# Attention over pooled maps and a large-kernel convolution: GpSimd's early 2x2 sums moved to the third chunk, partial products copied back two steps ahead

## The chip, the cores and the metric

The kernel runs on one core of a Trainium2 chip. The metric is the device time of one execution in microseconds (us). Four runs of the kernel before gave 3069.72 to 3074.2 us, with a median of 3070.95. All matrices are float32.

## The reference

The input x is 384 channels of 192x192. Two layers follow each other, each added to its input. `_gn` is a group norm over 32 groups of 12 channels, each over the whole image.

```
# layer 0
qkv = einsum(gn(x), w_qkv) + b_qkv          # 384 -> 3*384 channels, 192x192
qkv = max over 2x2 cells                    # 96x96
qkv = depthwise 3x3 convolution + b_dw
q, k, v = split; q, k normalized over the 96*96 positions
attn = einsum(q, k) per head (48x48, 8 heads)
out = sum of 4 softmaxes, each over the top 24, 32, 36, 38 of a row, times v
out = gelu(out), repeated 2x2, projected by w_proj + b_proj
x = x + out
# layer 1
x = x + sum of 7 depthwise convolutions of gn(x) (13x13 and smaller), each with its scale and shift
```

The change touches only the start of layer 0: the group norm's statistics, which need all of x, and the first products with w_qkv that are made while those statistics still run.

## The kernel before

**Stages.** (1) Statistics: all of x is read once and its mean and variance are taken by channel. (2) The main loop of layer 0: x is read again in bands of eight image rows (B, 24 bands, each in two halves sb of four rows), normalized, multiplied with w_qkv on TensorE (`project`, line 615), reduced by 2x2 maxima on VectorE (`pool`, line 627), and convolved 3x3 on VectorE (`taps`, line 663); q and k in a first pass, v in a second. (3) Attention and projection. (4) The large convolution on TensorE (line 1297). The stages from (1) to the end of (2) are written with a manual schedule: each engine executes its instructions in the order in which the program emits them. An engine that waits for a semaphore holds up everything behind it in its queue, DMA issues included.

**The statistics.** The first two bands (`NKEEP` = 2) come through the tiles `xts`. The rest of each chunk of 128 channels (chunks 1, 2 and 3 in this document, j = 0, 1, 2 in the code) is cut into NX = 22 pieces of 128x1536, so n = 0 to 65 counts the pieces of all three chunks, with j, b = divmod(n, 22): chunk 2 is n = 22 to 43, chunk 3 is n = 44 to 65. The loop over n does the following for each piece:
- It takes the piece's statistics: three `bn_stats` on VectorE (line 476), or, in chunks 1 and 2 for b = 4, 7, 10, 13, 16 and 19, two passes of ScalarE, one for the sum and one for the square (lines 472 and 473).
- It gives the piece's buffer back and issues the load of a later piece into the buffer that is the oldest free one (`load_blocks`, line 310). Eight such buffers go round, three in the memory of `v` and five called `xs`; so from n = 34 on, piece n takes the buffer that piece n - 8 has left (n = 26 to 33 take those of n - 12, since four pieces ahead of them go to places of their own). From n = 8 on, loads of even n are issued by SP, those of odd n by GpSimd.
- It advances the merging of the convolution weights on GpSimd (`merge`), and for each odd n it calls `sum_one`.

At the end of a chunk, `bn_aggr` (line 505) joins the statistics; for chunks 1 and 2 VectorE then reads what ScalarE has summed up (line 510).

**The early work.** With chunk 1's statistics done, the groups that lie in it are known, and its channels of early pieces can be normalized. `ready` (line 387) normalizes one piece of 128 channels by 4 image rows on ScalarE, and appends it to the list `early_sums`. `first_chunk`, advanced by one step after each `bn_stats` of chunk 2, normalizes the channels of chunk 1 of bands 2 to 5 and of both halves of bands 0 and 1, eight pieces, multiplies those of bands 2 to 5 with the q and k weights (m = 0, 1, 2; `multiply`, line 398) and copies each partial product from PSUM to SBUF (`put_by`, line 409). `early`, advanced in the same way in chunk 3, does so for the channels of chunk 2: eight more pieces, and 18 products (`EARLY`: bands 0 to 5, m = 0 to 2). For bands 0 and 1 (the first NKEEP * NJ = 6 steps) it multiplies both chunks at once. For bands 2 to 5 the product that was put by must be copied back into PSUM first (`fill`, line 246), the new one is accumulated on it, and the result is put by again. Once the group values are there, `early` emits all steps up to n = 15 without a pause and yields True, which sets `going`; the last two steps (LATE = 2) are emitted after the loop, around the statistics of the third chunk's groups. PSUM has two buffers of this kind (`qkvps`, bufs=2), which `multiply`, `fill` and the main loop's `project` share.

**The 2x2 sums.** Layer 1 needs 2x2 sums of the normalized x. `sum_one` takes the oldest entry of `early_sums` and calls `sum_up`: three additions on GpSimd (lines 257 to 259) into one of two small buffers at the end of `v`'s memory, taken in turn, and a DMA issued by GpSimd that writes 96 KB to `sums` (line 261). There are 16 entries in all. What is left after the loop is summed in `while early_sums: sum_one()`, which stands behind the nine memsets of the tiles `pooled` (line 578) and ahead of the main loop's own work for GpSimd.

**The end of the stage.** `group_stats` computes the last groups' mean and variance with small matmuls (lines 112, 123 and 147), a square root on ScalarE (line 90), and VectorE's steps between; then ScalarE normalizes the third chunk of band 0 (line 456), the first product is filled back (line 246), and the main loop begins on TensorE (line 615).

Of the kernel before, what the change touches and what calls it, by code (L numbers as in the profile page):

```python
# [16 lines left out]
NJ = C // P  # L17
# [40 lines left out]
def tile_attn_then_large_kernel_conv(ctx: ExitStack, tc: tile.TileContext, a: dict, out: bass.AP):  # L58
# [149 lines left out]
    NKEEP = 2  # L208
    EARLY = [(B, m) for B in range(6) for m in range(NJ)]
# [26 lines left out]
    def halved(t):  # L236
        return t.rearrange("p (r w) -> p r w", r=SR)

    filled = []

    def fill(B, m, sb):


        if sb == 0 and (B, m) in begun:
            ps = qkvps.tile([P, SR, 512], F32, tag="qkv", name="qkv")
            nc.scalar.copy(ps[:, :, : 2 * W], halved(begun[B, m]))  # L246
            filled.append(ps)
# [20 lines left out]
    with (  # L268
# [28 lines left out]
        def load_blocks():  # L297

            while waiting:
                n = waiting[0]  # L300
                j, b = divmod(n, NX)
                if (j, b) in kept:
                    xs = kept[j, b]
                elif ring:
                    xs = ring.pop(0)
                else:
                    return

                eng = nc.scalar if n < 8 else nc.gpsimd if n % 2 == 1 else nc.sync
                eng.dma_start(out=xs, in_=x[j * P : (j + 1) * P, FX + b * FB : FX + (b + 1) * FB])  # L310
                xss[waiting.pop(0)] = xs
                if len(xss) == 2:
                    yield
# [57 lines left out]
        def sum_one():  # L371
            if early_sums:
                t, B, sb, j = early_sums.pop(0)
                o = NJ * HS * WS - (len(early_sums) % 2 + 1) * SR * WS
                sum_up(free[:, o : o + SR * WS].rearrange("p (r w) -> p r w", r=SR), t, B, sb, j)


        def rows_stats(n):
            xt = xts[n // 2, n % 2]
            for j in range(NJ):  # L380
                nc.vector.bn_stats(stats[:, j, 2 * n, :], xt[:, j, :512])
                nc.vector.bn_stats(stats[:, j, 2 * n + 1, :], xt[:, j, 512:])

        def ready(B, sb, j):

            t = xts[B, sb][:, j] if B < NKEEP else kept[j, B - NKEEP][:, :HB]
            nc.scalar.activation(t, t, AF.Identity, bias=gn0[:, j, 1:2], scale=gn0[:, j, 0:1])
            early_sums.append((t, B, sb, j))
            pieces[B, sb, j] = t

        def multiply(B, m, js, ps=None):

            start = ps is None
            if start:
                ps = qkvps.tile([P, SR, 512], F32, tag="qkv", name="qkv")
            for r in range(SR):
                for j in js:
                    nc.tensor.matmul(  # L398
                        ps[:, r, : 2 * W],
                        lhsT=wqk[:, j, m * P : (m + 1) * P],  # L400
                        rhs=pieces[B, 0, j][:, r * 2 * W : (r + 1) * 2 * W],
                        start=(start and j == js[0]),
                        stop=(j == js[-1]),
                        skip_group_check=not start,
                    )
            return ps

        def put_by(B, m, ps):
            nc.scalar.copy(halved(begun[B, m]), ps[:, :, : 2 * W])
# [22 lines left out]
        def early():  # L432

            pc = yield from group_stats(s1, s_ps, mvx, "ge", gw, terms[1:6], (1,), True)
            yield
            nc.vector.tensor_copy(gn0[:, 1], pc[:, 1])
            ready(0, 0, 1)
            ahead = None
            for n, (B, m) in enumerate(EARLY):
                if m == 0 and B < EARLY[-1][0]:  # L440
                    ready(B + 1, 0, 1)
                ps = multiply(B, m, (0, 1)) if B < NKEEP else multiply(B, m, (1,), ahead)
                if n + 1 < len(EARLY) and EARLY[n + 1][0] >= NKEEP:
                    fill(*EARLY[n + 1], 0)
                    ahead = filled.pop()
                if n == len(EARLY) - 1:
                    yield True
                put_by(B, m, ps)
                if n < NKEEP:
                    ready(n, 1, 1)  # L450
                if n >= len(EARLY) - LATE - 1:
                    yield True
# [4 lines left out]

        early_sums, pieces = [], {}
        begin, first = first_chunk(), early()
        going = False  # L460
        pivot = s1.tile([P, 2, 2], F32, name="pivot")
        acc = s1.tile([P, 2, len(BY_ACT), 2], F32, name="acc")
        done = [NS0] * NJ
        for n in range(NJ * NX):
            if n in (1, 3, 5, 7):
                rows_stats(n // 2)
            j, b = divmod(n, NX)
            xt = xss.pop(n)
            if j < 2 and b in BY_ACT:

                sums2 = acc[:, j, BY_ACT.index(b)]
                nc.scalar.activation(xt, xt, AF.Identity, bias=pivot[:, j, 0:1], accum_out=sums2[:, 0:1])
                nc.scalar.activation(xt, xt, AF.Square, accum_out=sums2[:, 1:2])
            else:
                for q in range(FB // 512):
                    nc.vector.bn_stats(stats[:, j, done[j], :], xt[:, q * 512 : (q + 1) * 512])  # L476
                    done[j] += 1
                    if j == 1:
                        next(begin, None)
                    if j == 2 and not going:  # L480
                        going = next(first)
                if j < 2 and b == 0:
                    nc.vector.bn_aggr(pivot[:, j], stats[:, j, NS0 : done[j]].rearrange("p n s -> p (n s)"))
                    nc.vector.tensor_scalar(pivot[:, j, 0:1], pivot[:, j, 0:1], -1.0, None, ALU.mult)
            if (j, b) not in kept:
                ring.append(xt)
            for _ in load_blocks():
                pass
            next(merging, None)
            if n % 2 == 1:  # L490
                sum_one()
            if j < 2 and b == NX - 16:
                w = P * (j + 1)
                nc.scalar.dma_start(
                    out=spares[j], in_=x[w : w + MORE[j], :].rearrange("c (k n) -> (c k) n", k=P // MORE[j])
                )
                nc.scalar.dma_start(out=wqk[:, j, :C], in_=wqkv[:, j, :C])
            if j < 2 and b == NX - 6:
                k = HW * MORE[j] // P // 384
                sy = stats[:, j, -k:]  # L500
                for q in range(k):
                    nc.vector.bn_stats(sy[:, q, :], spares[j][:, q * 384 : (q + 1) * 384])
                nc.vector.bn_aggr(mvx[:, 3 * j, :], sy.rearrange("p n s -> p (n s)"))
            if b == NX - 1:
                nc.vector.bn_aggr(
                    mvx[:, (1, 4, 6)[j], :], stats[:, j, : done[j]].rearrange("p n s -> p (n s)")
                )
                if j < 2:
                    m = mvx[:, 3 * j + 2, :]
                    nc.vector.tensor_reduce(m, acc[:, j].rearrange("p n s -> p s n"), AX.X, ALU.add)  # L510
                    nc.vector.tensor_scalar(m, m, 1.0 / len(BY_ACT) / FB, None, ALU.mult)
                    t = s1.tile([P, 1], F32, name=f"sq{j}")
                    nc.vector.tensor_mul(t, m[:, 0:1], m[:, 0:1])
                    nc.vector.tensor_sub(m[:, 1:2], m[:, 1:2], t)
                    nc.vector.tensor_sub(m[:, 0:1], m[:, 0:1], pivot[:, j, 0:1])
# [24 lines left out]
    with ctx_v:  # L540
# [380 lines left out]
        with ctx_m:  # L921
# [4 lines left out]
            for s, (B, u, m, sb) in enumerate(steps):  # L926
# [8 lines left out]
                ps = project(B, m, sb)  # L935
                if s + 1 < len(steps):
                    n = steps[s + 1]
# [8 lines left out]
                if B + 1 < 2 * NB:  # L946
                    ahead = (u - 6,) if B < NB else (2 * u - 6, 2 * u - 5)
# [38 lines left out]
        with (  # L986
# [31 lines left out]
            with tc.manual_schedule():  # L1018
# [22 lines left out]
                for b in range(NBB):  # L1041
# [6 lines left out]
                    for c in range(NPR):  # L1048
                        k = P if c < NJ else P2
                        ps = b1_ps.tile([P, NBK], F32, tag=f"av{c}", name="av")  # L1050
# [293 lines left out]
        with (  # L1344
# [4 lines left out]
            with tc.manual_schedule():  # L1349
                for n in range(NJ * NBB):  # L1350
# [6 lines left out]
                    ps = b2_ps.tile([P, NBK], F32, tag="pj", name="pj")  # L1357
# [62 lines left out]
    with (  # L1420
# [5 lines left out]
        with tc.manual_schedule():  # L1426
# [4 lines left out]
            for k in range(NK):  # L1431
# [6 lines left out]
                for c in range(CC):  # L1438
# [13 lines left out]
                    n = c - (CC - 3 if k == 0 else 3)  # L1452
# [54 lines left out]
```

## Time and profile before

| | |
|---|---|
| median of 4 runs | 3070.95 us (3069.72 to 3074.2) |
| profiled execution, its time | 3070.8 us |
| its span in the profile | 3068.7 us |
| mean granted clock of TensorE | 0.993 |
| busy over the span: PE, DVE, ACT, POOL | 96%, 82%, 44%, 30% |
| first matmul of the main loop (line 615) | 177.66 us |
| 16 sums of early pieces, DMA issues (line 261) | 81.6 to 167.9 us |
| time from such an issue to its landing, least, median, most | 1.9, 5.9, 10.7 us |
| loads of line 310 from issue to landing, least, median, most | 4.4, 11.2, 26.4 us |

Times inside the execution count from the start of the span. PE is TensorE, PEld its loading of weights, DVE VectorE, ACT ScalarE, POOL GpSimd and SP the engine that issues most DMAs; a q behind a name (SPq, ACTq) is that engine's queue issuing a DMA. In lists in order of time, the first number is the start, the second the length. "a<-b" names what is written and what is read. The chain that ended last is followed back from the last instruction, at each step to what released it. Idle time ahead of an instruction is put down to the releaser that came last by the profile; where the engine named had long been done, it was another.

### The profile page before, as it was taken

Reading aid. Unit: us, or ns where it says so; the run is one execution under the profiler, and the core shown is the slowest. Engines: PE = TensorE matmul, PEld = TensorE weight load, DVE = VectorE, ACT = ScalarE, POOL = GpSimd, SP = SyncE. Lnnn points to the kernel's source line nnn. Section 1 sums busy time; section 2 is a strip of 40 time slices with the busy share of each in tenths; the row PEclk is TensorE's granted clock in tenths of the full one; section 3 lists DMA queues with packets and bytes.
Section 4 is the critical chain, followed back from the end, with each engine's and each line's share of the span. In section 5 each row is a group of like instructions: output and inputs, shape, how many; then the busy total and the mean of one; then the engine's idle time right before and its main releaser. Section 6 shows DMA issues by size and latency. Waiting matters only on the chain.

```text
span 3068.7 us, 32213 instructions
## 1 busy us (share of the span) xinstructions
PE 2932.4 (96%) x10842; PEld 1944.3 (63%) x10842; DVE 2515.9 (82%) x3483; ACT 1336.0 (44%) x2457; POOL 932.4 (30%) x1147
## 2 busy tenths in 40 slices
PE   0699999999999999999999999999999999999998
PEld 0355556666666666666555555555777877777776
DVE  6778897878888887888999899888788777777775
ACT  2655554444444444444444444733333333333332
POOL 4422132332323232412222222500433333333332
PEclk9899999999999999999999999999999999999999
DMA  9943342424333333333333332587999999999994
GB/s 386 379 158 95 131 155 77 154 88 146 96 134 102 132 114 120 128 107 110 103 101 101 129 105 70 170 230 205 267 268 243 245 243 245 245 244 246 245 220 118
DMA packets 275924, 525.73 MB, mean 171 GB/s; under 512 B 25954, under 2 KB 190480, under 8 KB 275632
## 3 DMA queue, kind: packets, MB, share of 16 engines
q1 hardware_dynamic: 204432, 326.44, 40.0%
q0 software_dynamic: 49376, 174.29, 17.5%
q10 hardware_dynamic: 21952, 22.95, 2.2%
q8 instruction: 86, 1.41, 0.2%
q14 instruction: 78, 0.64, 0.1%
HBM read 362.23 MB, written 161.37 MB: 171 GB/s over the span
## 4 chain that ended last, share of the span: by engine, by line
PE 84%; DVE 10%; DMA 3%; issue 2%; ACT 1%; POOL 0%; ACTq 0%; SPq 0%; POOLq 0%; DVEq 0%
PE qkv L615 45%; PE conv L1297 29%; PE pj L1359 4%; DVE v L663 3%; DVE acc L663 2%; PE av L1051 2%; DVE mx L627 2%; PE gram L704 2%; PE tr L692 2%; DMA v<-in_x 1%; DVE stats L476 1%; DMA xt<-in_x 1%; PE qkv L398 1%; DMA xs<-in_x 0%; DVE xp L1279 0%
## 5 line engine op out<-in xcount | busy, mean ns | idle before, releaser
L615 PE MATMUL qkv<-xt,wqk 128*128 128x384 f32 x3312 | 1087.6, 487 | 6.1 <-ACT qkv L246 5.5
L1297 PE MATMUL conv<-xp,wt 128*128 128x288 f32 (+1 forms) x3840 | 917.7, 402 | 2.2 <-ACT co L1305 2.2
L615 PEld LDWEIGHTS qkv<-xt,wqk 128*128 128x128 f32 x3312 | 621.1, 190 | 425.4 <-ACT qkv L246 12.2
L1297 PEld LDWEIGHTS conv<-xp,wt 128*128 128x128 f32 x3840 | 729.8, 190 | 187.8 <-ACT co L1305 2.6
L663 DVE SCALAR_TENSOR_TENSOR acc<-pooled,wd,acc 128x384 f32<-128x384 f32 (+2 forms) x1152 | 731.5, 635 | 30.5
L634 ACT ACTIVATE pooled<-mx,bq 128x192 f32<-128x192 f32 x432 | 196.8, 455 | 921.2 <-DVE mx L627 919.8
L627 DVE TENSOR_REDUCE mx<-qkv 128x192 f32<-128x768 f32 x432 | 412.1, 954 | 210.3 <-PE qkv L615 194.1
L1279 DVE STREAM_TRANSPOSE xp<-xn 128x4608 f32<-128x4608 f32 (+1 forms) x107 | 441.8, 4129 | 166.5 <-PE conv L1297 158.2
L615 PE MATMUL qkv<-xt,wv 128*128 128x384 f32 x1728 | 563.7, 487 | 1.7 <-ACT xt L596 1.1
L615 PEld LDWEIGHTS qkv<-xt,wv 128*128 128x128 f32 x1728 | 325.8, 190 | 234.1 <-ACT xt L596 7.5
L1305 ACT ACTIVATE co<-conv,cb 128x288 f32<-128x288 f32 x384 | 191.1, 499 | 598.8 <-PE conv L1297 588.6
L663 DVE SCALAR_TENSOR_TENSOR v<-pooled,wd,v 128x384 f32<-128x384 f32 (+2 forms) x576 | 375.4, 652 | 15.1
L257 POOL TENSOR_TENSOR sum<-xt 128x192 f32<-128x192 f32 x128 | 87.5, 684 | 957.1 <-ACT xt L596 944.6
L1322 POOL DMA_DIRECT2D out<-o x191 | 105.8, 583 | 569.3 <-DVE o L1313 514.5
L596 ACT ACTIVATE xt<-xt,gn 128x768 f32<-128x768 f32 x278 | 275.4, 1014 | 0.0
L1256 POOL TENSOR_TENSOR raw<-raw,up 128x2496 f32<-128x2496 f32 x46 | 230.8, 5017 | 24.6 <-DMA up<-pd 23.0
L1313 DVE STREAM_TRANSPOSE o<-co 128x2304 f32<-128x2304 f32 (+1 forms) x50 | 210.0, 4204 | 19.8 <-ACT co L1305 19.8
L732 POOL DMA_DIRECT2D zd<-v x96 | 72.0, 757 | 240.6 <-ACT v L723 239.9
L1359 PE MATMUL pj<-v,wp 128*128 128x384 f32 x432 | 142.5, 489 | 0.9 <-ACT gx L1062 0.6
L1359 PEld LDWEIGHTS pj<-v,wp 128*128 128x128 f32 x432 | 81.1, 190 | 55.5 <-ACT gx L1062 1.2
L1264 ACT ACTIVATE xn<-raw,par 128x2112 f32<-128x2112 f32 x48 | 102.9, 2144 | 3.3 <-POOL raw L1256 1.7
L258 POOL TENSOR_TENSOR sum<-sum,xt 128x192 f32<-128x192 f32 x128 | 100.9, 789 | 10.8
(284 smaller groups left out, 1918.0 us busy)
## 6 DMA issues: line engine op xcount, KB each, us to landing
xt<-in_x SPq DMA_DIRECT2D x96, 1152.0 KB, 7.6
wt<-zd SPq DMA_DIRECT2D x46, 1536.0 KB, 13.8
raw<-in_x SPq DMA_DIRECT2D x182, 312.0 KB, 13.8
out<-o POOLq DMA_DIRECT2D x188, 288.0 KB, 7.2
zd<-v POOLq DMA_DIRECT2D x96, 416.0 KB, 4.6
up<-pd SPq DMA_DIRECT2D x184, 156.0 KB, 12.5
xs<-in_x POOLq DMA_DIRECT2D x20, 768.0 KB, 10.6
smj<-sums SPq DMA_DIRECT2D x72, 192.0 KB, 3.0
```

Source lines behind the costliest of these rows:

```text
L596: nc.scalar.activation(xt[:, j], xt[:, j], AF.Identity, bias=gn0[:, j, 1:2], scale=gn0[:, j, 0:1])
L615: nc.tensor.matmul(ps[:, r, : 2 * W], lhsT=wq[:, j, mm * P : (mm + 1) * P], rhs=xt[:, j, r * 2 * W : (r + 1) * 2 * W], start=(j == 0), sto ...
L627: nc.vector.tensor_reduce(mx, ps[:, :, : 2 * W].rearrange("p r (y w x) -> p r w y x", y=2, x=2), AX.XY, ALU.max,)
L634: nc.scalar.activation(pool_t[m][:, k : k + SR, 1 : 1 + WS], mx, AF.Identity, bias=bq[:, m : m + 1])
L663: nc.vector.scalar_tensor_tensor(acc[:, :nt], pool_t[m][:, k0 + dy : k0 + dy + nt, dx : dx + WS], wd[:, m, t : t + 1], acc[:, :nt], ALU.mu ...
L1256: eng.tensor_add(rv, rv, uv.unsqueeze(2).to_broadcast([P, (m1 - m0) * WS, 2]))
L1279: nc.vector.transpose(bass.AP(at.tensor, at.offset, [list(at.ap[0]), [NBQ, n], [1, NBQ], [NQ * NBQ, CC], [ME * NBQ, NE]],), bass.AP(row.te ...
L1297: nc.tensor.matmul(ps[:, t0:t1], lhsT=wt[:, c, o : o + P], rhs=d[:, c, g + 2 * t0 : g + 2 * t1 - 1 : 2, :], start=(g == 1), stop=(g == NGR ...
L1305: nc.scalar.activation(co[:, c], ps, AF.Identity, bias=cb[:, cc : cc + 1])
L1313: nc.vector.transpose(bass.AP(at.tensor, at.offset, [list(at.ap[0]), [2 * W, n], [BC, NBQ], [W, 2], [1, BC]]), bass.AP(of.tensor, of.offse ...
L1322: engines[u % len(engines)].dma_start(out=bass.AP(out.tensor, out.offset + k * CC * HW + (2 * u + t0 * BR) * W, [[ME * UQ * W, CC * NE], [ ...
L1359: nc.tensor.matmul(ps, lhsT=wp[:, j, i * P : (i + 1) * P], rhs=v[:, j, b * RB : (b + 1) * RB, :].rearrange("p r w -> p (r w)"), start=(j = ...
```

## The change

There are two edits in the code of the statistics stage. The first adds a condition: `sum_one` is called for odd n only once `going` is set, that is from shortly after the start of chunk 3 on. The list of sums and their order stay; those that the loop doesn't reach are made after it. The second changes where `early` copies put-by products back into PSUM: in place of copying step n + 1's product ahead of the put-by of step n, it copies the product of step n + 2 after the put-by of step n, into the buffer that this has just left, and takes the filled buffers from the list `filled` in order. Numbers, sizes and operands of all instructions stay the same.

```diff
@@ -435,17 +435,17 @@
             yield
             nc.vector.tensor_copy(gn0[:, 1], pc[:, 1])
             ready(0, 0, 1)
-            ahead = None
             for n, (B, m) in enumerate(EARLY):
                 if m == 0 and B < EARLY[-1][0]:
                     ready(B + 1, 0, 1)
-                ps = multiply(B, m, (0, 1)) if B < NKEEP else multiply(B, m, (1,), ahead)
-                if n + 1 < len(EARLY) and EARLY[n + 1][0] >= NKEEP:
+                ps = multiply(B, m, (0, 1)) if B < NKEEP else multiply(B, m, (1,), filled.pop(0))
+                if n + 1 == NKEEP * NJ:
                     fill(*EARLY[n + 1], 0)
-                    ahead = filled.pop()
                 if n == len(EARLY) - 1:
                     yield True
                 put_by(B, m, ps)
+                if NKEEP * NJ - 1 <= n < len(EARLY) - 2:
+                    fill(*EARLY[n + 2], 0)
                 if n < NKEEP:
                     ready(n, 1, 1)
                 if n >= len(EARLY) - LATE - 1:
@@ -487,7 +487,7 @@
             for _ in load_blocks():
                 pass
             next(merging, None)
-            if n % 2 == 1:
+            if going and n % 2 == 1:
                 sum_one()
             if j < 2 and b == NX - 16:
                 w = P * (j + 1)
```

## The prediction

> **What bounds the kernel now.** I read the page first: TensorE is busy in nine tenths or more of every slice from the third on, so the edit, which lies in the first 178 us, can give only what brings the start of the main loop (the first matmul of line 615 at 177.66 us) forward. From there TensorE is back to back, so a microsecond before it is a microsecond of the whole. Then the chain that ended last, cut to 85-180 us (start, length, what):
>
> ```profile
> 96.87 0.20 ACT xs L473
> 97.06 0.28 issue
> 97.35 0.53 POOL xs L310
> 97.89 0.53 POOL v L257
> ...
> 106.63 0.58 POOL sums L261
> 107.21 3.64 issue
> 110.87 6.51 DMA xs<-in_x
> 117.40 1.89 DVE stats L476 x3
> 119.31 1.67 DVE mvx L505
> ...
> 156.19 0.57 POOL sums L261
> 156.75 8.30 DMA v<-in_x
> 165.08 1.89 DVE stats L476 x3
> 167.00 2.17 DVE mvx L505
> ...
> 177.66 1.57 PE qkv L615 x4
> ```
>
> Two waits for a load decide it: the last piece of chunk 2 (n=43, issued by GpSimd at 110.87, landed 117.40) and the last of chunk 3 (n=65, issued by GpSimd at 156.75, landed 165.08). The chain shows 2x2 sums ahead of both issues. But the 3.64 us of "issue" before 110.87 is a wait: n=43 takes the buffer of n=35, which ScalarE reads. The next view is the timelines of ScalarE and GpSimd there (start, length; in brackets idle time before and its releaser):
>
> ```profile
> 110.87 0.53 POOL L310 DMA_DIRECT2D xs<-in_x  x1 [3.66 <-ACT xs L473]
> ...
> 144.91 0.50 POOL L257 TENSOR_TENSOR v<-xt 128x192 f32<-128x192 f32 x1 [5.03 <-DMA sums<-v]
> ...
> 117.41 0.19 ACT L473 ACTIVATION_READ_ACCUMULATOR v<-v 128x1 f32 x1
> ```
>
> So the sums of chunk 2 don't set when n=43 is issued, and ScalarE's own part of chunk 2 ends at 117.60 whatever GpSimd does. Third, the stretches (length, busy PE, PEld, DVE, ACT, POOL, then clock, DMA share, GB/s) and VectorE's and TensorE's waits:
>
> ```profile
> 100.00:110.00 10.00, 6.37 (x23) 3.22 (x22) 6.68 (x13) 8.96 (x12) 6.20 (x11) 1.00 0.91 321
> 130.00:140.00 10.00, 9.91 (x24) 5.11 (x24) 10.00 (x19) 5.39 (x6) 6.16 (x11) 0.76 1.02 420
> ```
> ```profile
> DVE stats L476 <- DMA xs<-in_x: 9.6, 5, 6.2
> DVE stats L476 <- DMA v<-in_x: 7.1, 4, 3.7
> ```
> ```profile
> PE qkv L398 <- ACT qkv L246: 3.3, 6, 1.2
> ```
>
> The DMA engines are full at about 420 GB/s from 120 to 160 us and leave gaps at 80-120 us. VectorE waits 16.7 us for loads; by its timeline 2.6 us of that lie in chunk 3 (0.60, 0.78, 0.16 and 1.02, from 148 us on).
>
> **What the Trainium skill says.** (1) "DMA: Bandwidth & Descriptors", Issuing engines are not separate DMA queues: DMAs of all issuers run on the same 16 engines and interleave. The trace agrees: a load of 768 KB takes 4.4 us to land in the emptier stretch 66-89 us, 12 to 15 us when issued at 115-121 us. (2) "GPSIMD Engine Reference", Key points: GpSimd contends with VectorE where VectorE works in a two-port mode or with two SBUF inputs. Line 476 has one input, and its three cost 1.88 us at 95.04 (GpSimd idle) and 1.88 us at 117.40 (a sum beside): no contention to win back there. (3) "TensorE: Matmul & The Clock Gate", What's actually happening: the clock goes by free-running windows of 3413 ns. The trace agrees: granted 0.50 from 169 to nearly 176 us, full after it, so the multiply at 172.2 takes 2.9 us for four matmuls that take 1.6 at 175.6.
>
> **The change, part by part.**
>
> *Sums out of chunk 2.* In the trace 8 sums are issued at 79-120 us and 8 from 132 on. The order of the changed kernel on GpSimd has none before the load n=55, then five before n=65, five behind it, and six after the nine memsets of line 578. A sum is 0.51+0.59+0.60 us of adds, 0.30 of a wait and 0.58 of issue: with the gaps, 2.75 us. What stood behind them in GpSimd's queue are loads. By the buffer each takes and when its reader is done: n=37 needs ScalarE at 96.97, issued 97.35 (unchanged); n=39 needs a reader done at 87.2, 100.63 becomes 97.9; n=41 needs 89.0, 103.92 becomes 98.5; n=43 needs ScalarE at 110.48 (unchanged); n=45, n=47 and n=49 go from 114.15, 117.42, 120.70 to about 111.4, 111.9, 117.9. SP's queue keeps its order, and its loads n=40, 42, 44 at 104.3-105.3 wait for ScalarE.
>
> So n=43 isn't issued earlier, but it finds fewer transfers ahead of it. A load at 420 GB/s is 786 KB/420 = 1.9 us of all engines. n=37, 39 and 41 from 97.4 on are 5.6 us of work, done by about 104.5 instead of 111; n=40, 42, 44 follow and are done by 112; n=43 then takes 1.9 us plus some 2 us from issue to first arrival: landed at about 115.0, not 117.4. VectorE has its statistics at 116.9 and line 505 done at 118.6, where it was 120.95. ScalarE's 117.60 lies below that, just. Gain 2.3 us. Bounds: 0 if the transfer is no quicker; 120.95-117.8 = 3.1, where ScalarE's end takes over.
>
> *Chunk 3.* From there the order on VectorE is the same: 120.9 to 166.96 us is 46.1 us, of which 2.6 are waits for loads. The DMA engines have lost the work of 8 sum writes before the last load (16 minus 3 behind it were 13; now 5). A write took some 0.25 us of all engines by its packets, so 2 us, and the 0.9-share stretch at 100-110 us gives back about 1. That is 3 us of lead in transfers against 2.3 of lead in VectorE, so the waits shrink by little. GpSimd's chain in front of n=65 keeps its form: each sum waits for the landing of the sum two before it (144.91 and 154.04 in the trace), and five sums stand before it as five did. I take 1.0 of the 2.6 us; bounds 0 and 2.6.
>
> *Fill two steps ahead.* The order on ScalarE differs in three places only: at m=0 of pieces B=2, 3 and 4 the copy back comes before the normalization of line 387, not after it; and fill 17 moves from behind the square root at 172.67 to before it. TensorE's 3.3 us of waits for line 246 would go if ScalarE had room, but it is busy 18.86 of the 19.5 us from 148.1 to 167.6. So the early multiplies end perhaps 0.5 us sooner. They don't set the end: TensorE is done at 166.63 and waits 2.29 us for line 505. Price on the path 0. If statistics gain over 5.1 us (2.3+2.3+0.5), the early multiplies are late next. The moved fill 17 ran at 172.78, while ScalarE waited for TensorE's 175.17: nothing won. Two buffers stay filled across the pause; the next user is line 398 itself.
>
> *The six sums behind.* 6 x 2.75 = 16.5 us on GpSimd from about 178 us to 195. Queued behind them: clear of step 4 (180.53 before), then the strip writes, which wait for ScalarE until 210.48. Nobody waits for clear. The memsets stay ahead of the sums; ScalarE waits 1.2 us for them at 180.44, under TensorE's work. They need GpSimd free at some 173; five sums behind n=65 end near 169. VectorE is busy 12.7 of 20 us at 180-200, so a slower neighbour is hidden by TensorE; without that cover the bound is 6 x 1.7 = 10 us of shared ports. I take 0. Their buffer xt is reloaded at step 12, about 28 us in: no wait.
>
> *The tail* from 167.00 to 177.66 us stays: 10.7 us. Its clock can turn: if TensorE's idle time before it falls so that the window isn't slow, the 2.9 us multiply falls to 1.6, and with line 123 (1.45 us at half clock) up to 2 us go. If the phase is bad, up to 1.7 us come.
>
> **Sum.** -2.3 - 1.0 + 0 + 0 + 0 = -3.3 us. The profiled execution took 3070.8 us with a span of 3068.7, 2.1 around it; less 3.3 is 3067.5. The median of the four runs is 3070.95, 0.15 above: **3067.7 us**.
>
> **The rivals.**
> - *No change (3071).* The last load of chunk 2 waits for ScalarE's square anyway, and its landing is set by the full engines, so chunk 2 ends where it did. For it: the bracket at 110.87. Against it: the 0.91 share before. The four runs span 4.5 us, so this is near the forecast.
> - *All waits go (3063.4).* Chunk 2 ends at ScalarE's bound (3.1), chunk 3 loses all its waits (2.6) and the tail comes to run at full clock (1.8): 7.5 us. Against it: GpSimd's chain before n=65 is still there.
> - *Slower (3077).* The sums of chunk 3 land later, because more loads are queued ahead on GpSimd's own queue. Two such landings (10.0 us for the sum of 132.78, 7.0 for that of 144.91) stand before n=65. If each grows by d, n=65 comes 2d later; from d = 1.7 us on the 3.3 are eaten, at 4.7 us it costs 6. Against it: GpSimd's loads have only four buffers in turn, so no more can be queued than before.
> - *The fill counts (3067.2).* Only if the early multiplies were late; then its 0.5 us come on top. This lies inside the forecast.
>
> **Chances.** Forecast (0.8 to 5.7 us faster) 0.62, no change 0.20, all waits go 0.11, slower 0.07. A measurement of this kernel tells about 0.2%, 6.1 us, from no change. Faster by more than that: the third case and the upper end of the first with the clock, 0.17. Slower: the last case with what I can't name, 0.08. Within: 0.75. The range 3063.2 to 3072.6 leaves out the slower case and half of the fastest.
>
> **What would show it.** Right: no line 257 before 130 us; n=39 and n=41 issued by 99; n=43 issued near 110.9 and landed near 115; line 505 of chunk 2 done at 118.6; n=65 issued near 154; first line 615 near 174.4; TensorE's wait for line 246 gone while line 409 ends no more than 0.5 us sooner against its start. Wrong: n=43 landing at 117 still; sums landing later than 10 us; line 505 of chunk 3 no longer the last to release TensorE at the end; a new wait for line 578 or for xt after 178 us.

## The result, and the profile after

| | before | after |
|---|---|---|
| median | 3071.23 us (60 runs, 3066.4 to 3075.35) | 3066.83 us (42 runs, 3063.68 to 3069.11) |
| ratio after to before, 95% interval | | 0.9985 [0.9981, 0.9990] |
| profiled execution, its span | 3070.8, 3068.7 us | 3066.95, 3064.8 us |
| last load of chunk 2 (n=43), issued, landed | 110.87, 117.40 | 111.00, 115.47 |
| VectorE through with chunk 2 (line 510) | 120.90 | 118.97 |
| from there to line 505 of chunk 3 | 46.10 | 43.09 |
| line 505 of chunk 3 starts | 167.00 | 162.06 |
| from there to the first matmul of line 615 | 10.66 | 9.50 |
| first matmul of line 615 | 177.66 | 171.56 |
| main loop and attention, from there to the first matmul of line 1359 | 1808.5 | 1808.9 |

The change makes the kernel faster by 0.15%, some 4.6 us by the ratio. The gain lies ahead of the main loop: 1.9 us in chunk 2 and 3.0 us in chunk 3.

The chain of work of the kernel after, cut as it was for before (start, length, what):

```profile
97.50 0.50 POOL xs L310
98.05 0.50 POOL xs L310
98.55 0.53 POOL v L310
99.08 11.91 issue
111.00 4.44 DMA xs<-in_x
115.47 1.89 DVE stats L476 x3
117.38 1.67 DVE mvx L505
...
145.45 0.81 ACT v L409
146.28 0.80 ACT qkv L246
147.08 0.96 ACT v L387
...
162.69 1.56 PE qkv L398 x4
164.25 0.29 PE g_ps L112 x6
...
171.56 1.57 PE qkv L615 x4
```

The sums (lines 257 to 261) have left the chain at 97 to 107 us, and the three loads stand together. The load at 111.00 is n=43, issued when it was before, and landed after 4.44 us instead of 6.51. The second load of the chain before (156.75, n=65) is no longer in it. In chunk 3 the chain now runs over ScalarE's copies (lines 409 and 246) and TensorE's early products, which end at 164.25. VectorE's line 505, 2.16 us long, ends at 164.22, so the two now finish together.

VectorE's and TensorE's waits of the kernel after at 70 to 180 us (what waited for what: us in total, times, longest):

```profile
DVE stats L476 <- DMA xs<-in_x: 8.7, 2, 6.5
DVE stats L476 <- DMA v<-in_x: 3.5, 1, 3.5
```
```profile
PE qkv L398 <- ACT qkv L246: 3.5, 6, 0.9
```

VectorE's nine waits for loads have become three, and none of those left lies in chunk 3. TensorE's waits for line 246, which the second edit concerns, are as long as they were (3.3 us).

GpSimd's timeline of the kernel after (start, length; in brackets the idle time before and its releaser):

```profile
111.00 1.58 POOL L310 DMA_DIRECT2D xs<-in_x  x3 [11.92 <-ACT xs L473]
...
139.78 0.50 POOL L257 TENSOR_TENSOR v<-xt 128x192 f32<-128x192 f32 x1 [1.84 <-DMA sums<-v]
...
151.68 0.53 POOL L310 DMA_DIRECT2D v<-in_x  x1
```

n=43, n=45 and n=47 are issued in one go. The third sum, which must wait until the first sum has been written, waits 1.84 us for that where it waited 5.03, and n=65 is issued at 151.68 and not at 156.75. The stretches of the kernel after (columns as in the prediction):

```profile
100.00:110.00 10.00, 6.37 (x24) 3.14 (x22) 7.04 (x14) 8.96 (x12) 0.00 (x0) 1.00 0.99 385
```

At 100 to 110 us the DMA engines move 385 GB/s where they moved 321. This alone doesn't make n=43 land sooner: of two later versions of the kernel, one (e5) moves 337 GB/s there and lands n=43 after 4.4 us, another (e9) moves 395 and lands it after 6.8.

### The profile page after: what moved, and what is told of

Read it like the earlier page. It is cut to its first block, busy times and chain, and to the rows that moved or that the text cites. A ratio compares the mean times of both kernels' runs of the same rounds, so it can differ in the third digit from the quotient of the medians.

```text
span 3064.8 us, 32208 instructions
## 1 busy us (share of the span) xinstructions
PE 2930.9 (96%) x10842; PEld 1941.3 (63%) x10842; DVE 2517.4 (82%) x3483; ACT 1336.8 (44%) x2457; POOL 932.8 (30%) x1147
## 4 chain that ended last, share of the span: by engine, by line
PE 84%; DVE 10%; DMA 2%; issue 2%; ACT 1%; POOL 0%; ACTq 0%; SPq 0%; POOLq 0%; DVEq 0%
PE qkv L615 45%; PE conv L1297 29%; PE pj L1359 4%; DVE v L663 3%; DVE acc L663 2%; PE av L1051 2%; DVE mx L627 2%; PE gram L704 2%; PE tr L692 2%; DMA v<-in_x 1%; DMA xt<-in_x 1%; PE qkv L398 1%; DVE stats L476 1%; DMA smj<-sums 0%; DVE xp L1279 0%
## 5 line engine op out<-in xcount | busy, mean ns | idle before, releaser
L663 DVE SCALAR_TENSOR_TENSOR v<-pooled,wd,v 128x384 f32<-128x384 f32 (+2 forms) x576 | 375.4, 652 | 15.1
```

The costliest lines, as they stand in the source:

```text
L663: nc.vector.scalar_tensor_tensor(acc[:, :nt], pool_t[m][:, k0 + dy : k0 + dy + nt, dx : dx + WS], wd[:, m, t : t + 1], acc[:, :nt], ALU.mu ...
```

## The experiments

All of these are measured against the kernel before. The account that they lead to comes first, because one run alone tells little here: single runs of one kernel differ by 5 us and more. For each kernel the table has what its profile shows of two stages, as differences from the profile before: when line 505 of chunk 3 starts ("start"), and how long it takes from the first matmul of line 615 to the first of line 1359, which is the main loop with the attention ("loop"). The stretch between the two depends on the clock (see the question on the tail's clock) and is left out.

| kernel | sums: beside chunk 2, chunk 3, after it | n=43, issue to landing | line 510 to line 505 of chunk 3 | start | loop | both | ratio to before [95%] |
|---|---|---|---|---|---|---|---|
| before | 8, 8, 0 | 6.5 | 46.10 | 0 | 0 | 0 | 1 |
| after | 0, 10, 6 | 4.4 | 43.09 | -4.9 | +0.4 | -4.5 | 0.9985 [0.9981, 0.9990] |
| e1 | 0, 10, 6 | 4.7 | 43.09 | -4.1 | +0.3 | -3.8 | 0.9984 [0.9977, 0.9990] |
| e2 | 8, 8, 0 | 6.3 | 46.39 | +0.2 | +0.2 | +0.4 | 1.0002 [0.9994, 1.0010] |
| e3 | 0, 0, 16 | 4.5 | 43.09 | -4.5 | +4.1 | -0.4 | 0.9994 [0.9986, 1.0003] |
| e4 | 8, 0, 8 | 5.7 | 43.09 | -3.4 | +1.5 | -1.9 | 1.0000 [0.9992, 1.0008] |
| e8 (e4 again) | 8, 0, 8 | 8.1 | 43.09 | -1.3 | +1.5 | +0.2 | one execution |
| e5 | adds of 8, then as after | 4.4 | 44.13 | -2.9 | +0.5 | -2.4 | 0.9991 [0.9983, 0.9999] |
| e9 | writes of 8, then as after | 6.8 | 43.09 | -2.5 | +0.4 | -2.1 | 0.9987 [0.9979, 0.9995] |
| e6 | 8, 8, 0 | 6.4 | 46.94 | +0.8 | +0.2 | +1.0 | 0.9999 [0.9991, 1.0007] |
| e7 | 0, 10, 6 | 4.5 | 42.66 | -5.3 | +1.1 | -4.2 | 0.9987 [0.9981, 0.9994] |
| e10 | 8, 0, 8 in the main loop | 6.3 | 43.66 | -2.7 | +0.6 | -2.1 | 0.9997 [0.9989, 1.0005] |
| e11 | 0, 0, 16 in the main loop | 4.5 | 43.09 | -5.0 | +0.7 | -4.3 | 0.9990 [0.9984, 0.9997] |
| e12 | 0, 10, 6 in the main loop | 4.5 | 43.09 | -5.0 | +0.6 | -4.4 | 0.9986 [0.9979, 0.9992] |

One thousandth of the ratio is 3.1 us. In every row that has an interval, "both" lies within it. The intervals reach 1.4 to 3.1 us to each side, so this is no sharp test, but no third stage is needed to account for the times. The column "start" takes line 505 for the end of the stage. In some profiles TensorE comes to the last groups' sums (line 112) only after line 505 has ended: some 0.5 us after it in e1 and e4, 1.0 in e3 and 1.7 in e7. That much of "start" doesn't reach the main loop there.

**Which of the two edits?** e1 is the kernel before with the first edit alone, e2 the kernel after with the first edit taken back, so that the second stands alone.

```diff
 # e1, from the kernel before
-            if n % 2 == 1:
+            if going and n % 2 == 1:
 # e2, from the kernel after
-            if going and n % 2 == 1:
+            if n % 2 == 1:
```

> The kernel before with the condition on the sums alone; the copies back stay one step ahead. My theory: the sums' place makes the whole gain, since ScalarE has no room for the copies anyway. Then the statistics of chunk 2 are done (line 510) near 119.0 us, chunk 3's line 505 starts near 162.1, the main loop starts near 171.6 us, and the time is 4 to 5 us below before (as the changed kernel, within 1 us). Rival, both edits are needed: the early multiplies end later than 164.25 us, the last groups' statistics wait for TensorE, the main loop starts at 172.5 us or later and 1 us or more of the gain is missing.

> The kernel before with the copies back two steps ahead alone; sums run from chunk 2 on as before. My theory: nothing, within 0.5 us of before; the main loop starts at 177 to 178 us, and the multiplies of line 398 between 148 and 167 us take as long as before (18.8 us). Rival: TensorE's waits for line 246 (3.3 us) go and the tail is shorter by up to 1.2 us, so the time is 1 us or more below before.

Measured: e1 3066.86 us, e2 3072.49 us. The whole gain comes from where the sums stand, and the fill two steps ahead alone gives nothing. The chain of e1 shows how close TensorE is behind the statistics once the sums have moved:

```profile
164.08 1.56 PE qkv L398 x4
165.63 0.29 PE g_ps L112 x6
```

In e1 VectorE's line 505 of chunk 3 starts at 162.87 and ends at 165.03, and TensorE comes to the group sums (line 112) only at 165.63, 0.6 us later. In the kernel after it came 0.03 us later. But this isn't the missing second edit. From the first product of bands 2 to 5 that `early` makes to the group sums, TensorE takes 18.7 us in the kernel before and in e1, and 18.9 us in e2 and in the kernel after: with the copies two steps ahead this stretch is 0.2 us longer, not shorter. What makes e1 late lies ahead of it. The six products of bands 0 and 1 take 18.6 us in e1 and 17.8 in the kernel after, and the granted clock from 130 to 135 us is 0.63 and 0.87. All of this is below what the medians of e1 and after (3066.86 and 3066.83) can tell.

**Which chunk is relieved?** e3 makes no sum in the loop, so that all 16 stand behind the memsets. e4 makes the sums beside chunk 2 and none beside chunk 3; e8 is e4 once more, to see whether its profile repeats.

```diff
 # e3, from the kernel after
-            if going and n % 2 == 1:
-                sum_one()
 # e4 and e8, from the kernel after
-            if going and n % 2 == 1:
+            if not going and n % 2 == 1:
```

> The changed kernel with no sum at all beside the statistics: all 16 come after the loop. If the changed kernel's stage is now set by VectorE's own work and the early multiplies (line 505 of chunk 3 at 162.06 us without a wait for a load since 115 us, the multiplies done at 164.25), the sums beside chunk 3 cost nothing there: line 505 starts at 162.0 to 162.9, the main loop at 171.5 to 173.5, and the time is within 1 us of the changed kernel. Rival, the sums left beside chunk 3 still hold up n=65: the stage ends 1 us or more sooner. Second rival, 16 sums (44 us of GpSimd) beside the first steps of the main loop hold up its strips or the reload of the first band: the time is 2 us or more above the changed kernel.

> The changed kernel with the condition turned round: the eight sums of chunk 2 are made beside chunk 2, as before, and the eight that stood beside chunk 3 come after the loop, so no sum stands in front of the last loads of chunk 3. It tells the two gains apart. If the loads' lead from chunk 2 ended the waits of chunk 3: line 510 comes near 120.9 us as before, VectorE still waits 2 us or more for loads in chunk 3, and the main loop starts at 175 us or later. If GpSimd's chain of sums before n=65 made those waits: line 510 near 120.9, but VectorE waits under 0.5 us in chunk 3, line 505 starts near 164.4 and the main loop starts near 174 us.

> A second profile of the kernel with the sums turned round (beside chunk 2, none beside chunk 3), whose first profile was one of the two fastest of its 13 executions, 3.7 us under their median. If chance alone made the first fast, by TensorE's clock: the statistics end as in the first (line 505 near 163.6 us) and the missing time lies in windows of half clock later. If the first profile's statistics were the exception: VectorE waits for loads in chunk 3 here, and line 505 starts at 165 us or later.

Measured: e3 3070.19, e4 3071.76, e8 3070.29 us. e3 has the gain of the statistics (line 505 of chunk 3 4.5 us sooner) and loses 4.1 us in the main loop. The sums then lie beside line 663. Its group in e3, where it is line 661, from 9 to 46 us into the main loop (busy time, mean ns of one; the last number is idle time before), and TensorE's waits in the first 46 us:

```profile
L661 DVE SCALAR_TENSOR_TENSOR acc<-pooled,wd,acc 128x288 f32<-128x288 f32 x40 | 27.5, 687 | 1.1
```
```profile
PE qkv L613 <- ACT qkv L246: 2.5, 3, 1.0
PE qkv L613 <- DVE mx L625: 0.5, 2, 0.2
```

The same group in the kernel before and in the kernel after, over the same stretch:

```profile
L663 DVE SCALAR_TENSOR_TENSOR acc<-pooled,wd,acc 128x288 f32<-128x288 f32 x44 | 22.7, 516 | 1.2
```
```profile
L663 DVE SCALAR_TENSOR_TENSOR acc<-pooled,wd,acc 128x288 f32<-128x288 f32 x44 | 24.6, 560 | 1.2
```

Beside GpSimd's sums line 663 becomes slower: 516 ns with no sum, 560 with six, 586 with eight (e4), 687 with sixteen. With six TensorE waits no longer than before (0.5 us, for the first product), with eight 1.0 us more, with sixteen 2.5 us more (2.0 for line 246 and 0.5 for line 625, which is line 627 in the others). That it is VectorE's time that reaches TensorE, the timelines of e4 show, VectorE's first, then TensorE's:

```profile
194.64 2.83 DVE L663 SCALAR_TENSOR_TENSOR acc<-pooled,wd,acc 128x288 f32<-128x288 f32 x4
197.39 0.94 DVE L627 TENSOR_REDUCE mx<-qkv 128x192 f32<-128x768 f32 x1
```
```profile
200.30 3.17 PE L615 MATMUL qkv<-xt,wqk 128*128 128x384 f32 x9 [1.01 <-ACT qkv L246]
```

Four of line 663 take 2.83 us here and 2.17 in the kernel before. The 2x2 maximum behind them is late, ScalarE's line 634 and the copy of line 246 wait for it, and TensorE waits for that copy. Of e3's 4.1 us these waits explain 2.5. Most of the rest arises in the same place: when TensorE has made its first 148 matmul records of the main loop and the first transposes (line 692, here 690), it is 3.9 us behind the kernel before, and 4.0 at 220 us. The transposes wait 0.2 us for line 663. The 148 records take 48.5 us in one stretch in the kernel before, and 49.6 in five stretches in e3, so starting again after the four waits costs another 1.0 us. That leaves 0.4 us without a row of its own.

e4 and e8 have no waits for loads in chunk 3 although the sums are still beside chunk 2: both go from line 510 to line 505 in 43.09 us (e10, which has its sums in the same places beside the statistics, has one wait of 0.24 us and takes 43.66). The gain of chunk 2 is small or missing (line 510 comes 0.4 us sooner in e4 and 1.7 later in e8), and they pay 1.5 us in the main loop. e4's median doesn't show a gain. Its two profiles, the first of them of the second fastest of its 13 executions, account for 1.9 us faster and 0.2 slower, and its interval reaches 2.5 us to both sides, so whether it gains a microsecond can't be told.

**What in the sums is it: GpSimd's adds or the writes?** e5 is the kernel after with eight dummy sums beside chunk 2, three adds each and no write. e9 is the kernel after with eight writes of 96 KB beside chunk 2, issued by GpSimd to a spare place, and no adds. Both make all 16 real sums as the kernel after does.

```diff
 # both, from the kernel after
+            if not going and n % 2 == 1 and len(dummies) < len(early_sums):
+                dummy_one()
 # dummy_one of e5
+            nc.gpsimd.tensor_add(d, xv[:, :, 0, :, 0], xv[:, :, 0, :, 1])
+            nc.gpsimd.tensor_add(d, d, xv[:, :, 1, :, 0])
+            nc.gpsimd.tensor_add(d, d, xv[:, :, 1, :, 1])
 # dummy_one of e9
+            nc.gpsimd.dma_start(out=spare[:, o : o + SR * WS], in_=t[:, : SR * WS])
```

> The changed kernel with eight dummy sums added beside chunk 2, where those of before stood: the three additions each, without the write. It tells the place in GpSimd's queue from the transfers. If the queue alone made the gain of chunk 2: n=39 and n=41 are issued at 99.5 us or later again, n=43 lands near 117, line 510 near 120.5, and most of the 4.4 us is lost. If the eight writes made it: line 510 stays near 119.0 us and the time is within 1 us of the changed kernel. Half and half is what my working says: about 1 us of 3 by the queue, 2 by the writes, so line 510 near 119.7.

> The changed kernel with eight writes of 96 KB from GpSimd's queue beside chunk 2, to a spare place in memory and without additions, where the sums of before stood. With the adds alone n=43 still landed 4.4 us after its issue, as in the changed kernel, against 6.5 in the kernel before. If the writes slow the loads: n=43 lands 5.5 us or more after its issue, line 510 comes at 120 us or later, and chunk 3 has waits for loads again (43.09 us from line 510 to line 505 is the stretch without any). If neither adds nor writes do it alone, but both together: landing in 4.4 to 4.9 us, line 510 by 119.8, and the time within 1 us of the changed kernel.

Measured: e5 3069.2, e9 3068.48 us; the two intervals overlap, so it is the profiles that tell them apart. VectorE's last statistics of chunk 2, e5 first (n=43 issued at 112.08), then e9 (issued at 111.13):

```profile
116.51 1.88 DVE L488 BATCH_NORM_STATS2 stats<-xs 128x6 f32<-128x512 f32 x3 [3.02 <-DMA xs<-in_x]
```
```profile
117.93 1.88 DVE L485 BATCH_NORM_STATS2 stats<-xs 128x6 f32<-128x512 f32 x3 [4.07 <-DMA xs<-in_x]
```

With the adds alone n=43 lands after 4.4 us, as in the kernel after; with the writes alone after 6.8 us, as in the kernel before. The other kernels fall on the same two sides: 4.4 to 4.7 us without writes beside chunk 2, 5.7 to 8.1 with them. In e9 n=39 and n=41 were issued early (98.6 and 99.6), in e5 late (99.8 and 102.2). So it is the writes, and not the place of n=39 and n=41 in the queue, that hold up n=43. Nor is it enough that the loads ahead are done: n=42, the last load of chunk 2 ahead of it, lands at 113.4 us in the kernel before, 111.1 in the kernel after, 111.6 in e5 and 112.0 in e9. Whether the writes issued ahead of n=43 count or those right behind it (113.58 in the kernel before, 111.66 to 113.78 in e9) is not tested.

In chunk 3 it is the other way round. GpSimd's third sum, e5 first, then e9:

```profile
142.14 0.50 POOL L257 TENSOR_TENSOR v<-xt 128x192 f32<-128x192 f32 x1 [3.13 <-DMA sums<-v]
```
```profile
141.21 0.50 POOL L257 TENSOR_TENSOR v<-xt 128x192 f32<-128x192 f32 x1 [0.80 <-DMA sums<-v]
```

The first sum, which it waits for, lands 8.1 us after its issue with the adds (134.07), 5.8 with the writes (135.46), 6.8 in the kernel after (133.00) and 10.0 in the kernel before (134.95). The adds delay the loads behind them on GpSimd: n=45 and n=47 are issued at 114.5 and 116.9 in e5, at 112.2 and 113.3 in e9, by 112.6 in the kernel after. My reading is that loads that are issued later are still in transfer when the first sum is written; the sum lands later, GpSimd's later loads are held up by it, and VectorE's waits come back (0.57 and 0.24 us in e5, none in e9).

The end of that chain can be followed in all profiles. Counted from line 510, n=65 is issued after 35.9 us in the kernel before, 35.9 in e2 and 37.1 in e6, which have all the waits; after 34.0 in e5, which has some; and after 31.6 to 32.7 in e9, e1, e7, e12 and the kernel after, which have none. Its beginning is not shown. e5 and e9 differ in more than n=45 and n=47: VectorE is through with chunk 2 at 120.01 in e5 and only at 121.43 in e9, and a VectorE that comes 1.4 us later has less to wait for.

**Is the tail's clock worth anything?** The stretch from line 505 of chunk 3 to line 615 shrank by 1.2 us in the profile after. The stretches of the kernels before and after there, and one of the kernel after in the projection (after the length of the stretch: PE, PEld, DVE, ACT, POOL, then clock, DMA share, GB/s):

```profile
170.00:180.00 10.00, 8.80 (x28) 5.02 (x28) 2.47 (x14) 4.96 (x7) 4.24 (x9) 0.71 0.11 21
```
```profile
170.00:180.00 10.00, 9.40 (x29) 5.06 (x28) 1.92 (x2) 4.68 (x7) 9.07 (x17) 1.00 0.28 57
...
2090.00:2094.50 4.50, 4.50 (x11) 2.63 (x12) 2.24 (x6) 0.90 (x2) 0.00 (x0) 0.62 0.96 322
```

The profile before has a slow window in the tail, and there the first of the two late products takes 2.92 us for four matmuls; the profile after has none (1.56 us). But the profile after has a slow window in the projection, from about 2090.6 on for 3.4 us, which the profile before has not, and the projection took 2.4 us longer. To see whether the clock can be kept up, e6 adds three matmuls without a use ahead of the last group statistics to the kernel before; e7 adds thirteen ahead of those of chunk 2 and two ahead of the last to the kernel after.

```diff
 # e6, from the kernel before; e7 likewise with 13 and 2
+        for r in range(3):
+            nc.tensor.matmul(
+                warm[:, : 2 * W], lhsT=wqk[:, 0, :P], rhs=pieces[5, 0, 1][:, : 2 * W], start=True, stop=True
+            )
         last = group_stats(s1, s_ps, mvx, "g0", gw, terms[4:], (2,))
```

> The kernel before with three extra matmuls (2.3 us, written to a PSUM bank that nobody reads) in TensorE's idle time ahead of the last groups' statistics. It measures what the slow clock costs in the tail. If the clock made the tail 10.66 us in the kernel before against 9.50 in the changed one: no clock of 0.50 from 165 us on, the tail from the start of line 505 to the main loop is 9.5 us, and the time is about 1 us below before, so that this part of the changed kernel's profile isn't the sums' doing. If the tail is set by something else: 10 us or more, and the same time as before.

> The changed kernel with extra matmuls in TensorE's idle time: 13 (10.1 us) after the first chunk's products, 2 (1.6 us) ahead of the last groups' statistics, written to a PSUM bank that nobody reads. If the slow clock costs what the profiles show: line 123 of chunk 2's groups takes 1.2 us and not 2.3, the normalization of line 387 comes 1.2 us sooner after line 510, the first 48 records of line 398 take 18.5 to 17.8 us less what they lost at half clock, the tail is 9.5 us in every run, and the time is 1 to 2 us below the changed kernel. If TensorE's clock doesn't matter, because VectorE's statistics and ScalarE set the end: the same time as the changed kernel, within 0.6 us.

Measured: e6 3071.87 us, 0.9999 [0.9991, 1.0007]; e7 3067.75 us, 0.9987 [0.9981, 0.9994]. Neither differs from the kernel that it was made from. Both still have half the clock in a part of the tail (172.2 to 175.6 and 169.4 to 176.2 us), so they don't show what a tail without it is worth; they show that these matmuls don't buy it. In e7 the two matmuls ahead of the last statistics even stand in the way: line 505 ends at 163.85, they run from 164.15 on for 1.45 us, and the group sums come at 165.53. The thirteen did something in this one profile. Half the clock begins at 121.7 us there, and before 115 in the kernel after; line 123 of chunk 2's groups takes 1.85 us in place of 2.29, and the way from line 510 to line 505 is 0.4 us shorter.

**Do the sums behind the loop cost anything?** e10, e11 and e12 are e4, e3 and the kernel after without the sums behind the memsets. The sums that are left over are made in the main loop, where its other sums are made, from the pieces read again.

```diff
-        while early_sums:
-            sum_one()
+        early_sums.clear()
```

> The kernel with the sums turned round (eight beside chunk 2, none beside chunk 3), but with the other eight made by the main loop when it has those pieces in hand, not ahead of it: GpSimd has four at most near the main loop's start. That kernel lost 1.0 us of TensorE there, beside line 663 at 586 ns against 516. If the sums beside line 663 made it no faster than before: line 663 runs at 520 to 560 ns in the first 46 us, TensorE's wait of 1.0 us is gone, and the time is 2 us or more below before. If its statistics made it so (chunk 2 late, in most executions): no more than 1 us below before.

> No early sum at all beside the statistics, and the 16 made by the main loop, each with its own piece: four at its start, four with the second band, two with each band from the third to the sixth. Statistics as in the changed kernel (line 510 near 119, 43.09 us to line 505). If only a crowd of sums beside line 663 is dear: the time is within 1 us of the changed kernel, 2 us or more under the version with all 16 ahead of the main loop (3070.19). If each sum beside a two-input operation of VectorE costs, wherever it stands: 2 us or more above the changed kernel.

> The changed kernel with its six left-over sums made by the main loop, one or two with each of the first six bands, in place of ahead of it. In the changed kernel line 663 runs at 560 ns in the first 46 us against 516 before, and TensorE doesn't wait there. If its six sums cost nothing: within 0.6 us of the changed kernel. If they cost: 0.5 to 1.5 us below it. If a sum in the bands that TensorE waits in (1.2 us a band from the second on) is dearer than one at the start: 1 us or more above it.

Measured: e10 3070.03, e11 3068.98, e12 3067.13 us. e12 equals the kernel after: six sums behind the loop cost nothing that can be measured. Spread over the main loop, the sixteen sums of e11 add 0.7 us to it and not the 4.1 of e3, and TensorE has no wait there beyond the first. So by the profiles the price is that of sums packed beside the start of the main loop. The medians don't show it: the intervals of e11 and e3 overlap, and e11's median is 2.2 us above that of the kernel after, which its profile (-4.3 us beside -4.5) doesn't explain. e10 is inconclusive: its interval takes in both no change and the 2.1 us of its profile. None of these beats the changed kernel.

## Why the prediction was right, and where it was off

*Sums out of chunk 2: forecast -2.3 us, measured -1.9.* n=39 and n=41 were issued at 98.05 and 98.55, as worked out, and n=43 at 111.00, set by ScalarE. It landed at 115.47, where the forecast said about 115.0, and ScalarE's 117.73 stayed below. The size was right, but its reason was not enough: it counted the loads n=37 to n=42 that come ahead of n=43 as done earlier, and they were (n=42 landed at 111.1 in place of 113.4), but e9, which has n=39 and n=41 issued as early and n=42 landed at 112.0, lands n=43 as late as before. The writes that are gone are the cause, and the working for this chunk didn't count them. That its 2.3 came so near is in part luck. (One reading beside it was loose: loads issued at 115 to 121 us took 9.9 to 15.1 us to land, not 12 to 15. Nothing rests on it.) How a write of 96 KB, worth about 0.25 us of all engines by its packets, lengthens a load's landing by some 2 us is not shown by these traces.

*Chunk 3: forecast -1.0 us, measured -3.0.* This is the term that was mis-sized. The 2.6 us of waits went altogether, and with them 0.4 us more: in VectorE's timelines a `bn_stats` alone takes 0.69 us and six in a row 3.66, which is 0.69 and five times 0.59, so one that starts after a wait costs 0.1 us more than one in a row, and four such starts were gone. What failed is the step that set 3 us of lead in transfers against 2.3 us of lead in VectorE, and took the two landings in front of n=65 as they were. GpSimd's chain did keep its form, but its first landing shrank from 10.0 to 6.8 us, so that n=65 was issued 5.1 us sooner and not 2.8. What shortened that landing is likely the lead of GpSimd's loads n=45 and n=47, whose new times the prediction had worked out (111.4 and 111.9) and not followed any further: e5 takes most of that lead away and brings 0.8 us of waits back. No run takes away that lead alone, so this stays an inference. In chunk 3 the rival "all waits go" was right. Of its other parts, chunk 2 at ScalarE's bound didn't come, and the tail at full clock came in the profile and is not shown for the median.

*Fill two ahead: forecast 0, measured 0 (e2).* The sign named for it was wrong: TensorE's waits for line 246 didn't go (3.3 and 3.5 us), and the early multiplies don't end 0.5 us sooner for it but take 0.2 us longer. The reason given was right all the same, and should have led to another sign: ScalarE has no gap from 147 us on, and a copy that comes earlier in the order of a full engine doesn't come earlier in time. The cover, though, is used up. TensorE waited 2.29 us for line 505 before; after, the two end together, and the chain runs over TensorE and ScalarE's copies, which the prediction had named as a sign against itself. Any further gain of the statistics would be late there. The prediction had put that point at 5.1 us, and 4.9 were gained.

*The six sums behind: forecast 0, measured 0 to 0.4.* They ran from 174.57 to 191.66, near the forecast of 178 to 195. The cover named was TensorE's work, and it held for six (main loop +0.4 us, e12 the same time). The Trainium skill's "GPSIMD Engine Reference", Key points, which names two SBUF inputs as a case in which VectorE and GpSimd contend, is confirmed from both sides: line 663 has two such inputs and goes from 2.17 to 3.01 us for four beside sums, while `bn_stats`, with one input, takes 8.97 us for fifteen in a row in the kernel after, beside sums, and in e3, where none run.

*The tail: forecast unchanged, measured -1.2 in the profile.* In the profile 2.4 us more in the projection go against it. Slow windows of 3.4 us, the length that the Trainium skill gives ("TensorE: Matmul & The Clock Gate", What's actually happening), or of two such in a row stood in the tail before and in the projection after, by what these runs show without a tie to the edit: e1 and e7 have one in the tail. Taking 0 for both was right for the median: -1.9 - 3.0 + 0.4 = -4.5 us, against 4.6 by the ratio.

## What to carry over

When a helper engine issues loads between pieces of its own work, follow each load that comes earlier through to the last write that queues behind it: taking the sums out of one chunk was worth more in the next (3.0 us) than in the chunk itself (1.9). Work that is moved off a full memory stage costs nothing only as far as the next stage has room: by the profiles six sums beside two-input VectorE work were free, and sixteen took 4.1 us of the 4.5 that they had freed. And an earlier place in the order of an engine that had no gap gave nothing here.

## What the runs showed of the hardware

- Eight writes of 96 KB in some 40 us lengthened the landing of a load of 768 KB from 4.4-4.7 to 5.7-8.1 us. The adds before them did not (4.4).
- Line 663 (128x288, two inputs and one output in SBUF) takes 0.54 us alone and up to 0.77 beside 128x192 adds on GpSimd (2.17 and 3.08 us for four, the latter in e3).
- TensorE lost more than the waits themselves when it was held up four times: 148 matmul records took 48.5 us in one stretch (before) and 49.6 in five (e3).
- Two or three matmuls placed ahead of the tail didn't prevent half the clock some microseconds later (e7, e6). Thirteen placed ahead of chunk 3 put it off from before 115 us to 121.7 (e7, one profile).
